# Queueing the transposes of a layer norm behind a later gather in a four-layer graph network kernel

## The chip, the cores and the metric

The kernel runs on one core of one Trainium2 chip. The metric is the device time in microseconds (us) of one execution. Before the change the median of three executions is 5404.78 us.

The engines are called by their short names: PE is TensorE (matmuls and transposes; PEld is its loading of weights), DVE is VectorE, ACT is ScalarE, POOL is GpSimd, SP is SyncE, which here issues DMAs.

## The reference, cut to what matters

There are 16 independent batches (graphs) of 1024 nodes with 128 features, and an adjacency matrix of 1024 x 1024 for each, about 1.6% of it filled plus the diagonal. Four layers follow each other. In front of each the features are normalised, and each adds its result to them:

```python
h = jnp.maximum(_layernorm(x, axis=-1), 0.0)
x = x + _L2_gnn_ref(h, adj, ...)          # layers 0, 1 and 3 in the same way
```

Layers 0 and 1 multiply the adjacency matrix with the features and a small weight. Layer 2 consists of two passes; each computes for every edge a score from the features of its two ends, forms messages from scores and adjacency, and updates the node features. Layer 3 is an attention with a softmax over the neighbours. The norm that the change is about is the one between layers 1 and 2: its result `h` is needed as it is (nodes on partitions, called `xf`) and transposed (features on partitions, called `xT`).

## The kernel before, in words

**Tiling.** The 1024 nodes are eight tiles of 128, so a batch's features are one SBUF tile of 128 x 8 x 128. Layer 2 works only on the existing edges. For each pair of node tiles (36 pairs: 28 off the diagonal, 8 on it) there are "hot" matrices of zeros and ones that pick a pair's edges out; off the diagonal they have 320 columns, on it 480. A *gather* is a product of such a matrix with the node terms: four matmuls into one PSUM bank `pre` (line 1008). ACT and DVE turn it into a hidden row `hid` (lines 1024 and 1025), *dots* reduce it to scores `sc` (line 1041), and *scatter* and *messages* bring them back to the nodes (lines 1098 to 1137). `pre` has two banks, so a gather has to wait until DVE has read the one before the last.

**Rounds.** One pass of layer 2 over a batch is a round. It goes through nine groups of four pairs: diagonal group 0, seven groups off the diagonal, diagonal group 8. The second round of a batch starts with the four diagonal gathers of group 0, while the second half of the node update of the first round is still under way (`between`, which calls `update`: matmuls h line 343 and xn line 352, transposes tx line 359, the add on DVE at line 360, statistics, a power on POOL, and from line 1170 the transposes and the `split` into the terms `part`, lines 297 and 892 to 894). Group 2's gathers are the first that need the second half's terms.

**Three lanes.** While the rounds of batch b run (lane m, the method `main`), the last part of batch b-1 (lane c, `last`: update and layer 3) and the first part of batch b+1 (lane a, `first`: layers 0 and 1, the norm of layer 2, then `build`, which makes the hot matrices) run beside them. Each lane is a generator. A `yield` names a cost in units of about a microsecond. `weave` (line 1264) keeps for each lane the sum of its yields divided by the lane's total (`MAIN_US`, `FIRST_US`, `LAST_US`), and always advances the lane that is furthest behind. What stands between two yields is traced in one piece.

**What sets the order.** This traced order is a priority. Tile's scheduler then simulates the engines with a cost model and gives each engine a fixed queue: of the instructions that are ready in the simulation, the one traced first goes next. An instruction that the simulation takes to be ready early can so be queued ahead of one traced earlier. On the chip each engine works through its queue in that order. `tc.issue_after(ins)` adds, to each instruction traced in its block on the engine of `ins`, an order behind `ins` in that queue, with no wait for the end of `ins`. The rounds already use it once, in `dots`.

**Around the change.** In `first`, after layer 1 has written the sum `x` (products nb line 289, then o and x, lines 330 to 335), `pre_ln` is called (line 776). Its `normal` takes statistics on DVE (bn, lines 231 to 239), the power on POOL (line 242), one more step on DVE (line 249), and then eight activations on ACT (line 251) that write `s.xf`. After a yield of 2, `transposed` puts eight transposes on PE (line 259), four into one PSUM bank, each four followed by a copy on ACT (line 260). Lane a has a single PSUM bank in these batches. After another yield of 2, `kept` writes `xT` and `x` to memory with DMAs on SP's queue (line 721), and `build` starts, whose first matmuls use the same bank. The lane's yields are, in order: 7.8 for layer 0's own terms, 32 for its eight tiles, 2 for the count, 22 for layer 1, the norm's 2 and 2, and 45.9 for `build`: 113.7 in all.

```python
yield from lane.pre_ln(xt, f"2_{name}", dst=s.xf)
s.xT = self.kept(lane.hT, "xT", f"xT0_{b}")
s.x = self.kept(xt, "x", f"xk_{b}")
yield from self.build(s, has, name)
```

Of the kernel before, what the change touches and what calls it, by code (L numbers as in the profile page):

```python
# [13 lines left out]
AF = mybir.ActivationFunctionType  # L14
# [26 lines left out]


MAIN_US = 184.0
FIRST_US = 115.0
LAST_US = 70.0


# [4 lines left out]
def tile_four_gnn_layers(  # L52
# [22 lines left out]
    nc = tc.nc  # L75
# [106 lines left out]
    def flat(t):  # L182
        return t.rearrange("p t d -> p (t d)")
# [346 lines left out]
    class Edges:  # L530
# [197 lines left out]
        def first(self, b):  # L728
            s = self.next = Batch()
            lane, name = self.a, f"{b}"  # L730
            xt = self.work.tile([P, T, D], F32, tag="x", name=f"x_{b}")
            nc.sync.dma_start(xt, x[b].rearrange("(t p) d -> p t d", p=P))
            for _ in lane.layer0_own(xt, name):
                if b:
                    yield 1.3
            z, own = lane.z, lane.o
            yield 0


            s.adjT = self.dram.tile([N, N], F32, tag="adjT", name=f"adjT_{b}", bufs=3)  # L740
            has = self.work.tile([P, len(BUCKETS), P], FP8, tag="has", name=f"has_{b}", bufs=1)
            deg = self.work.tile([P, 2, T], F32, tag="deg", name=f"deg_{b}")
            rdeg = deg[:, 1]
            for t in range(T):
                at = self.load(
                    "a", adj[b, t * P : (t + 1) * P, :].rearrange("p (k n) -> p k n", n=P),
                    f"at_{b}_{t}",
                )
                ct = self.load("a", self.columns(adj[b], t), f"ct_{b}_{t}")
                turned = lane.scratch(f"tn_{b}_{t}")  # L750
                nc.scalar.activation(turned, at, AF.Copy, accum_out=deg[:, 0, t : t + 1])
                for ks, ps in lane.halves(f"tn_{b}_{t}"):
                    for i, k in enumerate(ks):
                        nc.tensor.transpose(ps[:, i], at[:, k], ident)
                    nc.scalar.activation(turned[:, ks[0] : ks[-1] + 1], ps, AF.Copy)
                    yield 1
                nc.sync.dma_start(self.columns(s.adjT, t), turned)
                parts = [(INDEX[t, t], t, t + 1)]
                if t + 1 < T:
                    parts.append((INDEX[t, t + 1], t + 1, T))  # L760
                for i, lo, hi in parts:
                    nc.vector.tensor_tensor(
                        has[:, i : i + hi - lo], ct[:, lo:hi], turned[:, lo:hi],
                        op=OP.logical_or, saturate=False,
                    )
                nc.vector.reciprocal(rdeg[:, t : t + 1], deg[:, 0, t : t + 1])
                lane.layer0_tile(t, ct, z, own, rdeg, name)
                yield 2
            lane.layer0_end(xt, own)
            self.count(s, has, name)  # L770
            yield 2
            yield from lane.layer1(
                xt, lambda t: self.load("a", self.columns(s.adjT, t), f"l1_{b}_{t}"), rdeg, name
            )
            s.xf = self.work.tile([P, T, D], F32, tag="xf0", name=f"xf0_{b}", bufs=1)
            yield from lane.pre_ln(xt, f"2_{name}", dst=s.xf)
            s.xT = self.kept(lane.hT, "xT", f"xT0_{b}")
            s.x = self.kept(xt, "x", f"xk_{b}")
            yield from self.build(s, has, name)

# [175 lines left out]
        class Group:  # L956
# [41 lines left out]
            def gather(self, i):  # L998

                path, c = self.path, self.c  # L1000
                t, u = self.grp[i]
                on, om = self.s.on[t, u], self.s.om[t, u]
                for d in range(self.nd):
                    pre = path.m.one(f"pre_{self.name}_{i}_{d}")

                    for v, node, hot in ((d, t, on), (1 - d, u, om)):
                        for k in range(2):
                            nc.tensor.matmul(  # L1008
                                pre[:, :c], path.parts[node // Q][:, k, node % Q, v], hot[:, :c],
                                start=(hot is on and k == 0),  # L1010
                                stop=(hot is om and k == 1),
                            )
                    if not self.diag:
                        hid = path.work.tile(
                            [P, 2, C_OFF], F16, tag="hid", name=f"hid_{self.name}_{i}_{d}", bufs=N_HID
                        )
                    elif i % 2 == 0:
                        self.two = flat(path.m.scratch(f"hid_{self.name}_{i}")).bitcast(F16).rearrange(
                            "p (i v c) -> p i v c", i=2, v=2
                        )  # L1020
                        hid = self.two[:, 0]
                    else:
                        hid = self.two[:, 1]
                    nc.scalar.activation(hid[:, 0, :c], pre[:, :c], AF.Relu)  # L1024
                    nc.vector.scalar_tensor_tensor(  # L1025
                        hid[:, 1, :c], pre[:, :c], 0.0, hid[:, 0, :c], op0=OP.max, op1=OP.subtract
                    )
                    self.hid.append(hid)
                    yield 0.6
# [203 lines left out]
        def run(self):  # L1233


            self.alone(self.a, "amcam")
            first = self.first(0)
            next(first)
            self.scaled()
            for us in first:  # L1240
                if us is None:
                    break

            self.alone(self.a, "")
            self.a.banks = [self.own["c"], self.own["a"]]
            self.next.builds = first
            done = None
            for b in range(B):
                s = self.next
                lanes = [(self.main(s, b), MAIN_US)]  # L1250
                if b:
                    self.a.banks = [self.own["a"]]
                    lanes.append((self.last(done, b - 1), LAST_US))
                if b + 1 < B:
                    lanes.append((chain(s.builds, self.first(b + 1)), FIRST_US))
                else:
                    self.c.banks = [self.own["c"], self.own["a"]]
                self.weave(lanes)
                done = s
            self.alone(self.c, "cmamc")  # L1260
            for _ in self.last(done, B - 1):
                pass
# [123 lines left out]
    with ExitStack() as stack:  # L1386
        path = Edges(stack)
# [16 lines left out]
    with tc.If(full > 0):  # L1404
        with ExitStack() as stack:
            path = Pairs(stack)
# [36 lines left out]
```

## Time and profile before

| what | value |
|---|---|
| time, three executions | 5400.31, 5404.78, 5408.11 us |
| span of the profiled execution | 5411.4 us |
| busy PE, DVE, ACT, POOL | 5012.4, 4288.8, 3055.3, 176.5 us |
| mean granted clock of PE | 0.978 |
| HBM read and written | 446.44 and 100.66 MB |
| transposes of this norm (line 259, `tp<-ident,xf`) | 128, median 0.421 us |
| their activations (line 251, `xf<-x,st`) | 128, median 0.478 us |
| power of the norms on POOL (line 242, 128x8) | 64, median 1.636 us |

Busy time is what an engine spent inside instructions; the rest of the span it waited. The list of waits tells for each engine and line how long it stood idle before such instructions and which instruction of which engine ended that wait. A wait for several things is put down to the one that came last. The timeline lists instructions in order of time, and those that follow each other on one engine with the same line are merged. The windows give busy times and the granted clock of PE (1.00 is full speed) in stretches that one chooses.

From batch 2 on the periods are much alike: from one batch's transposes of this norm to the next one's it is 325 to 332 us.

### The profile page before, as it was taken

The numbers are of one execution on the slowest core, as the hardware profiler recorded it, in microseconds if no ns is written. First come the engines' busy times: TensorE is split into PE (matmuls) and PEld (weight loads), VectorE is DVE, ScalarE is ACT, GpSimd is POOL, SyncE is SP. The second block draws the span as 40 slices with busy tenths as digits, with TensorE's granted clock in tenths as the row PEclk, the third lists the DMA queues.
The fourth block names the chain that finished last, engine by engine and source line by source line (L and its number), as shares of the span: only waits on it lengthen the run. The fifth ranks groups of instructions, "written<-read, shape, count | busy, mean of one in ns | idle before, by whom it ended". The sixth has DMA issues, their size and how long they took to land.

```text
span 5411.4 us, 113484 instructions
## 1 busy us (share of the span) xinstructions
PE 5012.4 (93%) x45109; PEld 3743.8 (69%) x45109; DVE 4288.8 (79%) x10567; ACT 3055.3 (56%) x6790; POOL 176.5 (3%) x137
## 2 busy tenths in 40 slices
PE   5999999999999999999999999999999999999986
PEld 4666767767776767767777677677767677677664
DVE  4776787877879788797877878778797787978876
ACT  4556464655646556465565656556465564655533
POOL 0000000000000000000000000000000000000000
PEclk8999999999999999999999999999999999999998
DMA  6242425243252423424234242432424334243121
GB/s 182 66 138 87 120 60 150 79 128 103 76 149 64 136 92 99 133 67 124 92 112 121 61 142 87 122 106 76 147 67 137 91 96 136 67 128 92 53 62 47
DMA packets 740139, 554.56 MB, mean 102 GB/s; under 512 B 32272, under 2 KB 686352, under 8 KB 739600
## 3 DMA queue, kind: packets, MB, share of 16 engines
q1 hardware_dynamic: 734496, 545.58, 33.6%
q8 instruction: 356, 5.83, 0.5%
q10 hardware_dynamic: 5104, 1.65, 0.1%
q14 instruction: 183, 1.50, 0.1%
HBM read 446.44 MB, written 100.66 MB: 101 GB/s over the span
## 4 chain that ended last, share of the span: by engine, by line
PE 61%; DVE 20%; ACT 10%; DMA 4%; POOL 2%; issue 2%; SPq 0%; ACTq 0%; POOLq 0%; DVEq 0%
PE pre L1008 15%; PE p L1120 7%; DVE val L1098 6%; PE nb L289 6%; PE msg L1137 5%; PE h L343 4%; PE hp L507 3%; PE bb L297 3%; PE sc L1041 3%; DVE hid L1025 3%; DMA at<-in_adj_dram 3%; PE pq L865 2%; PE pn L829 2%; POOL st L242 2%; ACT hid L1024 2%
## 5 line engine op out<-in xcount | busy, mean ns | idle before, releaser
L1024 ACT ACTIVATE hid<-pre 128x320 f16<-128x320 f32 (+1 forms) x2048 | 922.2, 456 | 713.5 <-PE pre L1008 679.5
L1025 DVE SCALAR_TENSOR_TENSOR hid<-pre,hid 128x320 f16<-128x320 f32 (+1 forms) x2048 | 1010.0, 505 | 262.7 <-ACT hid L1024 245.8
L1008 PEld LDWEIGHTS <-part 128*128 128x128 f16 x8192 | 752.7, 99 | 429.3 <-issue 211.4
L1008 PE MATMUL pre<-on,part 128*128 128x320 fp8e4 (+1 forms) x4096 | 966.6, 311 | 42.5 <-DVE hid L1025 32.3
L1008 PE MATMUL pre<-om,part 128*128 128x320 fp8e4 (+1 forms) x4096 | 979.0, 312 | 0.0
L1098 DVE TENSOR_TENSOR val<-onT,u 128x384 f32<-128x384 fp8e4 (+1 forms) x1152 | 603.3, 580 | 3.6
L1137 PE MATMUL msg<-upd,xf 128*128 128x128 f32 (+3 forms) x3008 | 591.8, 320 | 0.0
L1120 PE MATMUL p<-val,omT 128*128 128x128 f16 x6528 | 532.7, 219 | 31.6 <-DVE val L1098 27.2
L1120 PEld LDWEIGHTS <-omT 128*128 128x128 fp8e4 x6528 | 433.4, 96 | 109.6 <-issue 37.1
L1098 DVE TENSOR_TENSOR val<-omT,u 128x384 f32<-128x384 fp8e4 x896 | 442.7, 549 | 0.0
L1137 PEld LDWEIGHTS msg<-upd,xf 128*128 128x128 f32 x3008 | 411.6, 191 | 17.6 <-DVE upd L1128 0.9
L877 ACT ACTIVATE om<-pm 128x320 fp8e4<-128x320 f32 (+1 forms) x576 | 268.6, 466 | 274.5 <-PE pm L829 270.1
L1128 DVE SCALAR_TENSOR_TENSOR upd<-p,adj 128x512 f32<-128x512 f32 x512 | 349.0, 682 | 80.7 <-PE p L1120 76.7
L1120 PE MATMUL p<-val,onT 128*128 128x128 f16 x4480 | 370.9, 220 | 1.4 <-DVE upd L1128 1.4
L861 ACT ACTIVATE onT<-pn 128x384 fp8e4<-128x384 f32 (+1 forms) x576 | 298.4, 518 | 106.4 <-PE pn L829 98.4
L1062 ACT ACTIVATE srow<-sc,be_s,down 128x128 f32<-128x128 f32 (+2 forms) x512 | 256.3, 540 | 163.3 <-PE sc L1041 162.3
L507 PE MATMUL hp<-wh,e 128*128 128x129 f32 x2048 | 331.1, 287 | 16.7 <-DVE e L503 16.7
L1120 PEld LDWEIGHTS <-onT 128*128 128x128 fp8e4 x4480 | 305.2, 97 | 49.5 <-issue 14.9
L507 PEld LDWEIGHTS hp<-wh,e 128*128 128x128 f32 x2048 | 279.9, 195 | 51.5 <-issue 24.0
L1041 PE MATMUL sc<-hid,slide 128*32 128x320 f16 (+1 forms) x4096 | 272.4, 320 | 29.9 <-DVE hid L1025 28.5
L820 DVE TENSOR_SCALAR on<-far,wid 128x384 fp8e4<-128x384 f16 (+1 forms) x576 | 238.6, 427 | 60.0 <-PE pre L1008 52.2
L816 ACT ACTIVATE far<-iota_off,mid 128x384 f16<-128x384 f16 x448 | 275.6, 629 | 11.8 <-DVE on L820 11.3
(217 smaller groups left out, 8122.0 us busy)
## 6 DMA issues: line engine op xcount, KB each, us to landing
at<-in_adj_dram SPq DMA_DIRECT2D x128, 512.0 KB, 4.1
ct<-in_adj_dram SPq DMA_DIRECT2D x128, 512.0 KB, 4.5
adjT<-tn SPq DMA_DIRECT2D x128, 512.0 KB, 5.3
l<-adjT SPq DMA_DIRECT2D x128, 512.0 KB, 4.3
adj<-adjT SPq DMA_DIRECT2D x256, 256.0 KB, 3.5
a<-adjT SPq DMA_DIRECT2D x128, 384.0 KB, 3.2
adj<-adjT SPq DMA_DIRECT2D x448, 64.0 KB, 2.2
adj<-adjT SPq DMA_DIRECT2D x192, 128.0 KB, 2.9
```

Of the source, the lines that this page charges most:

```text
L289: nc.tensor.matmul(ps, mat[:, k], z[:, k], start=(k == 0), stop=(k == T - 1))
L507: nc.tensor.matmul(sums[:, t], e[:, i, t * P : (t + 1) * P], wh[:, k + i, : D + 1], start=False, stop=True, skip_group_check=True,)
L816: nc.scalar.activation(far[:, : ck * P], self.iota[t == u][:, : ck * P], AF.Abs, bias=s.mid[:, i : i + 1])
L861: nc.scalar.activation(onT, pn[:, : ck * P], AF.Copy, saturate=False)
L1008: nc.tensor.matmul(pre[:, :c], path.parts[node // Q][:, k, node % Q, v], hot[:, :c], start=(hot is on and k == 0), stop=(hot is om and k = ...
L1024: nc.scalar.activation(hid[:, 0, :c], pre[:, :c], AF.Relu)
L1025: nc.vector.scalar_tensor_tensor(hid[:, 1, :c], pre[:, :c], 0.0, hid[:, 0, :c], op0=OP.max, op1=OP.subtract)
L1041: ins = nc.tensor.matmul(self.sc[g * G : (g + 1) * G, : self.c], self.path.slide[:, self.l, G - 1 - r : 2 * G - 1 - r], self.hid[self.done ...
L1098: nc.vector.tensor_tensor(pair[:, i % 2, :ck], right[:, :ck], v.to_broadcast([P, ck, P]), op=OP.mult)
L1120: nc.tensor.matmul(self.ps[d][:, i], left[:, k], halves[:, k, :, h], start=(k, h) == terms[0], stop=(k, h) == terms[-1],)
L1128: nc.vector.scalar_tensor_tensor(upd, self.ps[d], S_SCALE, self.adj[:, d * Q : (d + 1) * Q], op0=OP.add, op1=OP.mult,)
L1137: nc.tensor.matmul(self.msg[h][:, (lo - h * Q) * P : (hi - h * Q) * P], self.xf[mb // Q][:, mb % Q], up, start=False, stop=True, skip_grou ...
```

## The change

The call of `pre_ln` is written out as its two parts. The yield between the norm and its transposes is 5 in place of 2, and the lane's total `FIRST_US` is 118 in place of 115. For all batches but the first, the transposes are traced inside `tc.issue_after(self.gathered)`; `gathered` is the last matmul of the gather that has been traced last. The copies on ACT are traced in the same block, but only instructions on PE get the edge.

```diff
-FIRST_US = 115.0
+FIRST_US = 118.0
...
-            yield from lane.pre_ln(xt, f"2_{name}", dst=s.xf)
-            s.xT = self.kept(lane.hT, "xT", f"xT0_{b}")
+            lane.normal(xt, s.xf, AF.Relu, f"2_{name}")
+            yield 5
+
+            with ExitStack() as behind:
+                if b:
+                    behind.enter_context(tc.issue_after(self.gathered))
+                turned = lane.transposed(s.xf, f"2_{name}")
+            yield 2
+            s.xT = self.kept(turned, "xT", f"xT0_{b}")
...
-                            nc.tensor.matmul(
+                            ins = nc.tensor.matmul(
...
+                    path.gathered = ins.ins
```

## The prediction

> **What bounds the kernel now.** I read the page first: busy shares, then the clock row, then the chain.
>
> ```profile
> PE 5012.4 (93%) x45109; PEld 3743.8 (69%) x45109; DVE 4288.8 (79%) x10567; ACT 3055.3 (56%) x6790; POOL 176.5 (3%) x137
> PE 61%; DVE 20%; ACT 10%; DMA 4%; POOL 2%; issue 2%; SPq 0%; ACTq 0%; POOLq 0%; DVEq 0%
> ```
>
> TensorE (PE) is the bound, and time can only be won where it stands still or runs at a reduced clock. DVE is second. Next I read the list of waits, PE and DVE rows. Columns: total us, times, longest.
>
> ```profile
> PE tp L259 <- ACT xf L251: 38.5, 15, 5.0
> PE pre L1008 <- DVE hid L1025: 32.3, 51, 2.8
> PE sc L1041 <- DVE hid L1025: 28.5, 22, 1.8
> PE pre L1008 <- DVE part L894: 3.8, 15, 1.0
> DVE st L249 <- POOL st L242: 98.0, 63, 1.8
> ```
>
> The first row is the step that moves: 15 waits, of which one of 4.96 us is batch 0's, alone at the start, and 14 are of 2.39 to 2.40 us, one in each of batches 2 to 15 (batch 1 has none). 14 x 2.39 = 33.5 us. The timeline of batch 3 around one of them (start us, us, engine, line; in brackets idle before):
>
> ```profile
> 970.07 0.83 PE L507 MATMUL hp<-wh,e 128*128 128x129 f32 x6
> 971.67 0.43 PE L1008 MATMUL pre<-on,part 128*128 128x320 fp8e4 x2 [0.76 <-DVE hid L1025]
> 971.94 0.43 PE L1008 MATMUL pre<-om,part 128*128 128x320 fp8e4 x2
> 974.76 0.33 PE L259 MATMUL tp<-ident,xf 128*128 128x128 f32 x1 [2.39 <-ACT xf L251]
> 975.02 0.38 PE L1041 MATMUL sc<-hid,slide 128*32 128x480 f16 x2
> 975.33 0.33 PE L259 MATMUL tp<-ident,xf 128*128 128x128 f32 x1
> ...
> 974.01 0.17 DVE L249 SCALAR_TENSOR_TENSOR st<-st 128x8 f32<-128x8 f32 x1 [1.41 <-POOL st L242]
> 974.30 0.64 DVE L1025 SCALAR_TENSOR_TENSOR hid<-pre,hid 128x480 f16<-128x480 f32 x1
> ```
>
> See two things. PE waits 0.76 + 2.39 = 3.15 us in this stretch. And DVE is held too: L249 waits 1.41 us for the power on POOL, and the hidden row that the next scores (sc) need stands behind L249 on DVE and ends at 974.94. The transposes hide a second wait that ends 0.2 us later. The clock by single microseconds (PE, PEld, DVE, ACT, POOL busy, then PEclk):
>
> ```profile
> 974.00:975.00 1.00, 0.24 (x1) 0.14 (x1) 0.99 (x5) 0.79 (x3) 0.00 (x0) 1.00 0.00 0
> 977.00:978.00 1.00, 1.00 (x6) 0.54 (x5) 0.86 (x4) 1.00 (x4) 0.10 (x1) 0.50 0.02 8
> 979.00:980.00 1.00, 1.00 (x7) 1.00 (x5) 0.96 (x3) 0.41 (x1) 0.00 (x0) 0.50 0.63 191
> ```
>
> After the stop PE is at half clock for 3.4 us here; taken over 10 us windows around all 14 stops, the half-clock stretches add up to 75.1 us (eight stretches of 6.8 us, six of 3.4). At half clock the same work takes double, so they cost 37.5 us.
>
> **What the Trainium skill says.** "TensorE: Matmul & The Clock Gate", What's actually happening: the clock is halved after an idle window of about 3.4 us and comes back after a busy one. The trace agrees in size: halves come in steps of 3.4 us behind these stops, though the stop here is 3.15 us in two pieces. The same page, Architectural detail, says that ACT and DVE are strict first-in first-out and that PE only pulls weight loads ahead: so one unready transpose stops all matmuls behind it, and L249 stops the hidden row. The timeline shows both. I use no price from the skill.
>
> **The change, part by part.** No instruction is added or removed: 128 transposes (median 0.421 us in this place, 0.273 for the same form elsewhere), 32 copies, the same DMAs. What changes is the order in which the planner sees them.
>
> (a) The yield of 5 in place of 2 and FIRST_US 118 in place of 115. The first lane's total rises from 113.7 to 116.7, so its end stays where it was (0.989 of the batch both times). Adding the yields up to the norm gives 63.8: 63.8/115 = 0.555 of the batch before, 63.8/118 = 0.541 after. The last neighbour product (L289) goes from 0.537 to 0.524. The norm and all before it therefore come up to 1.4% of a batch sooner relative to the rounds: 0.014 x 327 us (the batch period in the windows between stops) = 4.6 us. The transposes are seen at 68.8/118 = 0.583 in place of 65.8/115 = 0.572, 3.6 us later.
>
> (b) The edge. At 0.583 the rounds have just issued the fourth diagonal gather of the second layer (0.578); before, it would have been the third (0.557). In the trace of before the transposes already come after the fourth (969.26) and one more (971.67). So the edge is a floor that keeps the planner from pulling the transposes up with the norm; by itself it does not move them down.
>
> What it gives: before 0.537 the last product waits behind the second diagonal gather and the update matmuls (h L343 1.88 us, gather 0.8, hp 0.7 in the PE timeline from 960.45 to 963.65); now it is seen ahead of them, so it can start some 3.2 us sooner. DVE has room: it is busy 0.22 to 0.48 of each microsecond from 962 to 966, and 1.00 from 968 on. Everything that hangs on it (o 1.24, x 1.22, bn 1.63, pow 1.64, ACT 0.50) moves with it, and the first transpose becomes ready near 974.7 - 3.2 = 971.5. PE is free from 970.9. The stop falls from 3.15 us to 0.6, and with a rest of the hidden-row wait I take 1.0. Bounds: 0 saved if the product cannot start sooner; 3.15 saved if all goes.
>
> Sum: 14 x 2.15 = 30 us of stop. Of the 37.5 us of half clock I take half, 19 us, since a stop of 1.0 us is well under a window but some batches lose the clock anyway (batch 1 does with 1.0 us of stop in the 5 us before its transposes). Together 49. Not all arrives at the end: between stops, the eight periods behind a 6.8 us half stretch average 328.7 us, the five behind 3.4 us 327.5; a difference of 1.2 for 1.7 us of lost PE work, so about 0.7 passes through. 0.7 x 49 = 34 us, 0.6%. Ceiling: 44.2 + 37.5 = 82 us, 0.7 of it 57, all of it 5329 in the profile.
>
> (c) The rest at nothing: the two copies (0.6 us) and the copy of xT to memory move later by 3 to 4 us. SyncE issues it at 980.21 and the next thing behind it that anyone needs soon is the load at 990.37; its reader is in the next batch. The single bank of lane a is held later, and the building of the hot matrices starts at 0.600 in place of 0.590; their readers are a batch away, and the lane's end is unmoved, which hides it. POOL has 3% of work.
>
> The profile's span, 5411.4, is 6.6 over the median 5404.78 of the timed runs (5400.31 to 5408.11). 5411.4 - 34 = 5377; against the median 5404.8 - 34 = **5370 us**.
>
> **The rivals.** *DVE's wait takes its place* (same). If the norm does not move up on DVE, L249 still waits 1.41 us for POOL, the hidden row still ends at 974.94, and PE waits for sc in place of the transpose: 0.2 us more of stop, then 0.4 saved because the scores are no longer paced by ACT. Within 5 us of 5404. For it: the two waits end 0.2 us apart. Against it: DVE stands idle from 964.5 to 965.6 in front of the chain.
>
> *The second half's update is pushed back* (slower). DVE's queue after the last product holds 1.24 + 1.22 + 1.63 + 0.6 us of the norm and a wait of 1.41. The add L360 (968.82) that heads the update of half 1 stands between them; it leads over xf, xfT (L1170), bb and part (L894, ending 989.4) to the gathers of group 2, and PE already waits for part 15 times, 3.8 us: no slack. If the norm's bn and L249 are now put ahead of L360, part comes up to 3.5 us later, in 14 batches 49 us, less the stop that is saved anyway (0.7 x 33): 5404 + 26 = 5430. It decides from the point where L360 starts after L249. For it: the norm is seen at 0.541, and the update's step that holds L360 at 0.552. Against: L360's input comes from PE at 968.7, after the moved bn would have run.
>
> *The edge and the pace do nothing to this stop* and only the new phase of lane a against the rounds counts: its transposes tn and products nb (L289), eight steps of each kind per layer, stand up to 1.4% of a batch elsewhere. Stops of PE elsewhere in a batch (0.5 to 1.5 us each, ten of them in batch 3) may go either way: 5404 plus or minus 15.
>
> **How the numbers follow.** Forecast 0.60, its own range 5340 to 5394 (ceiling with 0.8 passing through, down to a gain of 0.2%). DVE's wait instead 0.15, 5394 to 5416. Update pushed back 0.15, 5416 to 5450. Phase only 0.10, split 0.03 faster, 0.02 same, 0.05 slower. Faster 0.63, same 0.17, slower 0.20; 0.2% (11 us) is about what a measurement of this kernel can tell from no change. A range that leaves no more than 2 in 10 out takes the forecast's, the whole of the second case and part of the third: 5338 to 5425.
>
> **What would show it.** Right: the row of tp waiting for ACT xf falls from 38.5 us to under 15 (5 of them are batch 0's), half-clock stretches behind these places fall from 75 us to under 45, the last nb of layer 1 starts before the second diagonal gather, L249 ends before the fourth gather's hidden row. Wrong: PE waits for sc or pre on DVE hid grow by what tp loses (first rival), pre waits for part grow from 3.8 us (second), or the period between stops stays at 327 us with the stop gone (third).

## The result, and the profile after

The changed kernel takes **5337.48 us** (median of 4 executions, 5336.17 to 5341.52), where the kernel before takes 5403.35 in the same comparison: a ratio of 0.9879, 95% interval 0.9861 to 0.9896. That is 66 us less; 34 were forecast. The direction is right; the time lies half a microsecond below the predicted range. The profiled execution spans 5339.7 us, 71.7 less than that of before.

The page after, busy time by engine and then the chain that ended last by engine:

```profile
PE 4962.4 (93%) x45109; PEld 3720.1 (70%) x45109; DVE 4286.7 (80%) x10567; ACT 3065.2 (57%) x6790; POOL 176.5 (3%) x137
PE 58%; DVE 23%; ACT 10%; DMA 5%; POOL 2%; issue 2%; ACTq 0%; SPq 0%; POOLq 0%; DVEq 0%
```

The same 45109 matmuls keep PE busy 50.0 us less (5012.4 before), and PE's time outside them falls by 21.7 (399.0 to 377.3). DVE and ACT do the same work in the same time. Next the list of waits after (total us, times, longest); the lines have moved by 7 or 8, so L1015, L1033, L1049 and L901 are L1008, L1025, L1041 and L894 of before:

```profile
PE pre L1015 <- DVE hid L1033: 33.7, 68, 2.8
...
PE tp L259 <- ACT hT L260: 23.1, 14, 1.7
...
PE pq L872 <- ACT onT L868: 21.5, 57, 0.6
PE tp L259 <- ACT xf L251: 20.4, 15, 5.0
...
PE sc L1049 <- DVE hid L1033: 17.5, 21, 1.8
...
PE pre L1015 <- DVE part L901: 3.8, 15, 1.0
...
DVE st L249 <- POOL st L242: 74.6, 63, 1.8
```

The row that was to fall did fall, from 38.5 to 20.4 us, of which 5 are batch 0's. But a row is new that the transposes of before did not have at all: 14 waits for `hT`, the copy on ACT, up to 1.7 us each, 23.1 in all. Together the two make 43.5 us, so the stop has changed its name and not its size. The waits for the hidden row have not grown by it (pre 32.3 to 33.7, sc 28.5 to 17.5) and pre for part is unmoved at 3.8. The largest fall elsewhere is that of `pq` (a product in `build`), which in before waited 39.1 us for `onT`, up to 1.5 us at once.

The timeline after, batch 3, PE and then ACT and DVE (start us, us, engine, line; in brackets idle before):

```profile
956.08 1.95 PE L289 MATMUL nb<-z,l 128*128 128x128 f32 x16
...
959.58 0.57 PE L1015 MATMUL pre<-on,part 128*128 128x480 fp8e4 x2
...
965.29 0.57 PE L1015 MATMUL pre<-om,part 128*128 128x480 fp8e4 x2
966.96 0.33 PE L259 MATMUL tp<-ident,xf 128*128 128x128 f32 x1 [1.10 <-ACT xf L251]
...
968.50 0.43 PE L1015 MATMUL pre<-om,part 128*128 128x320 fp8e4 x2
970.59 0.55 PE L259 MATMUL tp<-ident,xf 128*128 128x128 f32 x3 [1.65 <-ACT hT L260]
971.70 0.88 PE L1049 MATMUL sc<-hid,slide 128*32 128x480 f16 x8 [0.57 <-DVE hid L1033]
...
966.41 3.18 ACT L251 ACTIVATE xf<-x,st 128x128 f32<-128x128 f32 x8 [1.55 <-DVE st L249]
969.50 0.55 ACT L1032 ACTIVATE hid<-pre 128x480 f16<-128x480 f32 x1
969.96 0.58 ACT L260 ACTIVATE hT<-tp 128x512 f32<-128x512 f32 x1
...
966.21 0.17 DVE L249 SCALAR_TENSOR_TENSOR st<-st 128x8 f32<-128x8 f32 x1 [1.11 <-POOL st L242]
966.30 0.65 DVE L1033 SCALAR_TENSOR_TENSOR hid<-pre,hid 128x480 f16<-128x480 f32 x1
```

The last product of layer 1 (956.08) does start ahead of the second diagonal gather (959.58), as predicted. The first transpose is ready 2.1 us after the start of the fourth diagonal gather (966.96 against 964.88), where it was 5.5 us after it before (974.76 against 969.26): 3.4 us nearer, and 3.2 were worked out. Yet the stop is now 1.10 + 1.65 + 0.57 = 3.32 us. The 1.65 us are spent on the lane's single bank: the first four transposes are done at 968.52, but their copy stands in ACT's queue behind activations 5 to 8 of `xf` and a hidden row. It starts at 969.96 and ends at 970.54, and only then may the second four start.

### The profile page after: what moved, and what is told of

Read it like the earlier page. It is cut to its first block, busy times and chain, and to the rows that moved or that the text cites. A ratio compares the mean times of both kernels' runs of the same rounds, so it can differ in the third digit from the quotient of the medians.

```text
span 5339.7 us, 113330 instructions
## 1 busy us (share of the span) xinstructions
PE 4962.4 (93%) x45109; PEld 3720.1 (70%) x45109; DVE 4286.7 (80%) x10567; ACT 3065.2 (57%) x6790; POOL 176.5 (3%) x137
## 3 DMA queue, kind: packets, MB, share of 16 engines
q10 hardware_dynamic: 5104, 1.65, 0.1%
## 4 chain that ended last, share of the span: by engine, by line
PE 58%; DVE 23%; ACT 10%; DMA 5%; POOL 2%; issue 2%; ACTq 0%; SPq 0%; POOLq 0%; DVEq 0%
PE pre L1015 15%; DVE val L1106 8%; PE p L1128 7%; PE nb L289 6%; PE msg L1145 5%; DMA at<-in_adj_dram 4%; PE sc L1049 3%; DVE hid L1033 3%; PE h L343 3%; PE bb L297 3%; PE pn L836 2%; PE hp L507 2%; PE pq L872 2%; ACT hid L1032 2%; POOL st L242 2%
## 5 line engine op out<-in xcount | busy, mean ns | idle before, releaser
L1033 DVE SCALAR_TENSOR_TENSOR hid<-pre,hid 128x320 f16<-128x320 f32 (+1 forms) x2048 | 1009.1, 505 | 232.9 <-ACT hid L1032 219.0
L1015 PEld LDWEIGHTS <-part 128*128 128x128 f16 x8192 | 748.3, 98 | 433.5 <-issue 210.4
L1015 PE MATMUL pre<-on,part 128*128 128x320 fp8e4 (+1 forms) x4096 | 971.8, 309 | 42.9 <-DVE hid L1033 33.7
L1015 PE MATMUL pre<-om,part 128*128 128x320 fp8e4 (+1 forms) x4096 | 972.7, 309 | 0.0
L1145 PEld LDWEIGHTS msg<-upd,xf 128*128 128x128 f32 x3008 | 406.5, 191 | 15.4 <-DVE upd L1136 1.7
L507 PEld LDWEIGHTS hp<-wh,e 128*128 128x128 f32 x2048 | 274.5, 195 | 36.6 <-DVE e L503 23.1
L876 DVE TENSOR_TENSOR omT<-pq,odd_off 128x384 fp8e4<-128x384 f32 x448 | 248.1, 554 | 55.6 <-PE pq L872 49.9
L1049 PE MATMUL sc<-hid,slide 128*32 128x320 f16 (+1 forms) x4096 | 269.6, 316 | 21.7 <-DVE hid L1033 17.5
L289 PE MATMUL nb<-z,ct 128*128 128x128 f32 x2048 | 267.6, 282 | 23.5 <-ACT tn L755 15.9
```

Of the source, the lines that this page charges most:

```text
L289: nc.tensor.matmul(ps, mat[:, k], z[:, k], start=(k == 0), stop=(k == T - 1))
L507: nc.tensor.matmul(sums[:, t], e[:, i, t * P : (t + 1) * P], wh[:, k + i, : D + 1], start=False, stop=True, skip_group_check=True,)
L1015: ins = nc.tensor.matmul(pre[:, :c], path.parts[node // Q][:, k, node % Q, v], hot[:, :c], start=(hot is on and k == 0), stop=(hot is om a ...
L1033: nc.vector.scalar_tensor_tensor(hid[:, 1, :c], pre[:, :c], 0.0, hid[:, 0, :c], op0=OP.max, op1=OP.subtract)
L1049: ins = nc.tensor.matmul(self.sc[g * G : (g + 1) * G, : self.c], self.path.slide[:, self.l, G - 1 - r : 2 * G - 1 - r], self.hid[self.done ...
L1145: nc.tensor.matmul(self.msg[h][:, (lo - h * Q) * P : (hi - h * Q) * P], self.xf[mb // Q][:, mb % Q], up, start=False, stop=True, skip_grou ...
```

## The experiments

All ratios are to the kernel before, run in the same comparison, with 95% intervals.

**The edge alone, the pace alone.** In `e2_no_edge` the edge is taken from the changed kernel. In `e1_pace_only` the yields of 2 and 5 are exchanged too, so that the norm comes as early as in the changed kernel and the transposes right behind it; FIRST_US stays 118 and `build` stays where the change put it.

```diff
-                if b:
+                if False:
```

and in e1 besides

```diff
-            yield 5
+            yield 2
...
-            yield 2
+            yield 5
             s.xT = self.kept(turned, "xT", f"xT0_{b}")
```

> Lane a's total is 118 and its yields add up to the same sum as in the changed kernel, but the 3 extra units stand after the transposes (norm, 2, transposes, 5) and there is no edge: the norm and all before it come sooner, the transposes do not come later. Theory P (the pace of lane a against the rounds makes the gain): ratio to before 0.988, half-clock time in the steady batches near the changed kernel's. Rival E (the transposes queued later make it): ratio 0.998 to 1.002 and the 2.4 us stop with its half clock is back.

> The changed kernel without the order behind the gather; yield of 5 and 118 kept. Theory P: ratio 0.988, since from batch 2 on the transposes come out behind the same gather anyway. Rival E: ratio 0.995 or more, as the transposes are pulled up to where ACT has not yet written their input.

Measured: e1 0.9858 (0.9838 to 0.9878), 5329.93 us; e2 0.985 (0.983 to 0.9871), 5327.21 us. The whole gain is there without the edge and without the later transposes. Compared as fixed queues, e2 differs from the changed kernel in batch 1 alone: from batch 2 on the edge orders nothing that the priorities did not order already. The edge alone, on the kernel before, was not run.

**The later transposes alone, the pace alone in its other half.** `e3_late_only` is the changed kernel with FIRST_US back at 115; `e4_first118` is the kernel before with 118.

```diff
-FIRST_US = 118.0
+FIRST_US = 115.0   # e3, on the changed kernel; e4 is the reverse, on the kernel before
```

> The changed kernel with the lane's total back at 115: the norm is traced at 0.555 of the batch as before the change, the transposes at 0.598 and with the edge. Theory P: ratio 0.997 to 1.003. Rival E: ratio 0.988 to 0.992.

> The kernel before with only the lane's total raised from 115 to 118; yields as before, so the lane's end comes at 0.964 of the batch in place of 0.989. Theory P: ratio 0.986 to 0.991, most of the gain from one number. Rival E: ratio 0.998 to 1.002. If what counts is that the lane's end stays at 0.989, the ratio is 0.995 or worse.

Measured: e3 0.9908 (0.9889 to 0.9926), 5357.4 us; e4 0.9914 (0.9895 to 0.9933), 5358.58 us. Each half gives some 0.9%, both together 1.2 to 1.5%. e3 lies in rival E's range and outside theory P's, e4 a hair above P's and outside E's: neither theory holds alone. In e3 the stop is a different one. Its timeline on PE:

```profile
965.17 0.43 PE L1015 MATMUL pre<-on,part 128*128 128x320 fp8e4 x2 [0.77 <-DVE hid L1033]
965.45 0.43 PE L1015 MATMUL pre<-om,part 128*128 128x320 fp8e4 x2
968.51 0.59 PE L1049 MATMUL sc<-hid,slide 128*32 128x480 f16 x8 [2.63 <-DVE hid L1033]
...
969.73 1.06 PE L259 MATMUL tp<-ident,xf 128*128 128x128 f32 x4
```

The transposes now wait for nothing, and PE waits 2.63 us for the hidden row that stands behind L249 on DVE. That is the mechanism of the first rival (the sc row goes from 28.5 to 63.1 us), and still the kernel is 48 us faster than before in the same comparison. The stop has changed hands there and hardly its length, so a shorter stop is not where the time comes from.

**Is it the wait for POOL?** If L249 is what holds DVE, DVE should not do it. In `e6_before_free_dve` (on the kernel before) and `e7_pace_free_dve` (on e1), DVE scales without waiting and POOL multiplies with its own power.

```diff
-            nc.vector.scalar_tensor_tensor(less, mean2, -0.5, rstd, op0=OP.mult, op1=OP.mult)
+            nc.vector.tensor_scalar(less, mean2, -0.5, None, op0=OP.mult)
+            nc.gpsimd.tensor_tensor(less, less, rstd, op=OP.mult)
```

> The kernel before, but the norm's last small step no longer waits on DVE for POOL's power: DVE scales the mean by -0.5 without waiting, and POOL multiplies it with the power; ACT then waits for POOL directly. Theory D (DVE held behind that step is the second lock of the stop, as seen by scores waiting for the hidden row): the DVE wait for POOL at that line (98 us) goes, but the transposes come later by POOL's second operation (about 1 us), so the stop before the transposes grows to 3 us or more; ratio 0.995 to 1.003. If the wait on DVE costs nothing: ratio 1.002 to 1.006.

> The pace-only kernel with the same freed DVE. Theory D: where the transposes are no longer last, freeing DVE pays: 2 to 5 us a batch less, ratio 0.978 to 0.984. If DVE's wait is hidden there: ratio 0.985 to 0.990.

Measured: 1.0006 (0.9997 to 1.0015) and 0.9857 (0.9841 to 0.9873), the latter against 0.9858 for e1. e6 lies in theory D's range, but e7 does not: freeing DVE pays nothing there either. In e6 PE still waits for `xf` 41.2 us (38.5 before): the chain to the transposes is no shorter.

**Is it the clock?** Fill matmuls on data that is ready when the stop begins stand ahead of the transposes in the kernel before (not in batch 0): they write a bank that the first transpose overwrites. One more line, not shown, keeps the variance that they read. Five, one, and two of them:

```diff
+                if h == 0 and b:
+                    for _ in range(N_FILL):
+                        nc.tensor.matmul(
+                            flat(ps)[:T], lane.var, flat(xt)[:, :HALF], start=True, stop=True
+                        )
                 for i, t in enumerate(ts):
                     nc.tensor.transpose(ps[:, i], s.xf[:, t], ident)
```

> The kernel before, with five more matmuls (8 columns of the norm's variance against 512 columns of x, into the bank that the first transposes then overwrite) queued right in front of the norm's transposes in batches 1 to 15. Their input is ready when the stop begins (variance written at 972.2 in batch 3, transposes start at 974.8), so they keep PE at work in the stop and shorten nothing. Theory C (more than half of the gain is the clock that is kept): half-clock time around the stops falls from 5.4 us a batch to under 2.5 and the ratio is 0.993 to 0.996. Rival (the gain is the idle time and the order, the clock is a by-product): ratio 0.999 or above, as the work only grows by about 2 us a batch.

> As the run with five filling matmuls, but with one (two halves of about 0.43 us each). From batch 2 on the queues of all engines are those of the kernel before, but for this matmul, which stands between the last gather and the transposes. It takes nothing off the stop: the transposes start when they did, only PE's longest idle stretch falls from 2.4 to 1.5 us. Theory C (the clock): half-clock time in the steady batches falls from 8.1 us to 3 to 6, and with 0.54 us of period per us of half clock (the slope between batches of the kernel before) the ratio is 0.9945 to 0.9985. Rival (idle time and order alone): ratio 0.9995 to 1.001.

> Two filling matmuls: the longest idle stretch falls to about 0.8 us. Theory C: half-clock time falls to 2 to 4 us a batch, ratio 0.992 to 0.996. Rival: ratio 1.000 to 1.002.

Measured: e5 0.9986 (0.9979 to 0.9993); e9 0.9988 (0.9982 to 0.9995); e10 0.9984 (0.9976 to 0.9991). All three lie between the ranges of the two theories. Five fills were too many: they ran 4.46 us, longer than the stop. For the clock, here are stretches of 2 us behind the stop, before and then e10, where the stop lies 3.0 us earlier (length, busy PE, PEld, DVE, ACT, POOL, then PEclk, DMA share, GB/s):

```profile
976.00:978.00 2.00, 2.00 (x11) 1.13 (x12) 1.10 (x5) 2.00 (x6) 1.10 (x1) 0.71 0.01 4
978.00:980.00 2.00, 2.00 (x11) 1.85 (x9) 1.97 (x6) 1.25 (x3) 0.00 (x0) 0.50 0.49 147
```

```profile
974.00:976.00 2.00, 2.00 (x15) 1.29 (x13) 1.87 (x7) 2.00 (x6) 0.09 (x1) 1.00 0.18 46
976.00:978.00 2.00, 1.20 (x15) 0.98 (x14) 1.97 (x6) 1.25 (x5) 0.00 (x0) 1.00 0.96 306
```

The half clock behind the stop is gone, in this batch and in the others: near the stop it is 5.36 us per batch before, 0.73 with one fill and none with two. Over whole batches, e9 and e10 have some 5 us less of it each, and e10's whole trace has as much half clock as the changed kernel's (154.4 us both, 241.6 before). That is worth 0.12 to 0.16%, 6 to 9 us. In the order of the kernel before, a kept clock is a real gain and a small one. The trace of e10 shows what holds it down:

```profile
977.01 0.66 PE L1185 MATMUL tp<-ident,xf 128*128 128x128 f32 x4 [0.80 <-DVE xf L374]
```

These are the transposes of the second half of the node update (L1170 before; L374 is the last step of that update on DVE, L371 before). With the clock kept PE comes to them sooner, but DVE ends the update when it did: 22.9 us after the start of the hidden row that opens the second round, in both kernels (means of the rounds of batches 2 to 14). So PE stands still for 0.80 us, and the transposes start at 22.9 where they started at 23.7. The fills therefore say what the clock is worth in the old order. What it is worth in the changed one, where DVE ends this update earlier, no run tests.

**Further along, and once more.** `e8_pace121` is e1 with 121 and a yield of 8 behind the transposes. `e11_pace_only_again` and `e12_changed_again` repeat e1 and the changed kernel in one comparison of five rounds.

> Pace only, one step further: lane total 121 and 8 units after the transposes. If an ever earlier lane a is better (trend): ratio 0.975 to 0.982. If 118 is one phase among several that avoid the long stop: ratio 0.984 to 0.994.

> The pace-only kernel once more beside the changed kernel on one chip. If the later queueing and the edge add nothing or cost a little: ratio 0.985 to 0.987, below that of the changed kernel by 0.001 to 0.003. If they help: above the changed kernel's.

> The changed kernel itself on the same chip as the others: ratio 0.987 to 0.989.

Measured: e8 0.9872 (0.9856 to 0.9889); e11 0.9867 (0.9852 to 0.9882), 5330.42 us; e12 0.9878 (0.9863 to 0.9893), 5337.36 us. The pace without the edge is as good as the change, and the better of the two each time by 7 to 8 us, though within the intervals.

**A scan of one number.** The kernel before with FIRST_US alone at 114, 116, 121 and 124.

```diff
-FIRST_US = 115.0
+FIRST_US = 114.0   # 116.0, 121.0, 124.0
```

> The kernel before with FIRST_US 114 alone: every step of lane a is seen up to 0.9% of a batch later against the rounds. Theory trend (earlier steps of lane a are better, 0.29% of time for each unit of FIRST_US, from 115 to 118): 1.003. Theory phase (the order of the queues at 115 happens to be a poor one, and neighbours of either side are better or like it without an order): 0.986 to 1.000, below 0.998 the likelier. A ratio above 1.001 speaks for the trend.

> The kernel before with FIRST_US 116 alone: steps of lane a up to 0.9% of a batch earlier. Theory trend: 0.997. Theory phase: no order, 0.988 to 1.004; a value at or below 0.991, a third of the way to 118 with all of its gain, speaks for the phase.

> The kernel before with FIRST_US 121 alone. Theory trend: 0.983, twice the gain of 118. Theory phase: 0.986 to 1.000, not better than 0.9914 of 118 by more than 0.004 except by chance, since the steady part of the gain of 118 came from one place behind the norm's stop (3.5 us per batch) that can't be won twice.

> The kernel before with FIRST_US 124 alone. Theory trend: 0.974. Theory phase: 0.986 to 1.002. A value above that of 118 contradicts the trend.

The table sets the scan beside the others. The last five columns are from the traces, in us per batch: the mean of 13 periods (from the end of this norm's transposes in batch 2 to their end in batch 15), PE's idle time and the half clock in it, and near these transposes the idle time (stretches that end between 4 us ahead of the first transpose and the end of the last: the stop) and the half clock (from 1 us ahead of the first to 5 us behind the last).

| kernel | ratio | period | PE idle | half clock | stop | half clock near it |
|---|---|---|---|---|---|---|
| FIRST_US 114 | 0.9986 (0.9976 to 0.9996) | 327.00 | 18.33 | 6.56 | 4.18 | 5.50 |
| before, 115 | 1 | 328.18 | 17.97 | 8.12 | 3.16 | 5.36 |
| 116 | 0.9954 (0.9937 to 0.997) | 326.34 | 17.08 | 3.41 | 2.09 | 1.95 |
| 118 (e4) | 0.9914 (0.9895 to 0.9933) | 325.01 | 17.88 | 2.10 | 2.30 | 1.69 |
| 121 | 0.993 (0.9913 to 0.9947) | 325.32 | 17.55 | 2.63 | 1.15 | 0.42 |
| 124 | 1.0153 (1.0132 to 1.0173) | 333.40 | 21.46 | 7.09 | 1.69 | 2.98 |
| changed, 118 | 0.9879 (0.9861 to 0.9896) | 323.29 | 16.50 | 2.17 | 3.32 | 2.19 |
| pace only, 118 (e1) | 0.9858 (0.9838 to 0.9878) | 322.87 | 16.41 | 2.10 | 2.30 | 1.85 |
| late only, 115 (e3) | 0.9908 (0.9889 to 0.9926) | 324.80 | 15.91 | 3.68 | 2.72 | 3.04 |

Read it against the stop. 121 has the smallest stop and almost no half clock near it, and is no faster than 118. 124 has about half the stop of before and is 1.5% slower. The changed kernel has the largest stop but one and the shortest time but one. The half clock alone does not order the kernels either: 118, the changed kernel and pace only have 2.1 to 2.2 us of it per period, and their periods lie 2.1 us apart. And FIRST_US has a valley rather than a slope, with its floor at 118 to 121: the trend's figures failed at 114, 121 and 124, and the phase's range held at 114, 116 and 121 and failed at 124. The waits of the kernel with 121 say the same in lines:

```profile
PE tp L259 <- ACT hT L260: 16.0, 14, 1.1
...
PE tp L259 <- ACT xf L251: 5.0, 1, 5.0
```

Only batch 0's wait for `xf` is left there (5.0, once): the row is where the prediction wanted it, and the time is 28 us above that of the changed kernel. With 124 other waits grow, from 32.3 and 15.4 us before:

```profile
PE pre L1008 <- DVE hid L1025: 56.5, 71, 2.9
PE pn L829 <- ACT om L877: 39.1, 97, 0.7
```

They are part of the 3.5 us by which PE's idle time per batch rises; why that order is so much worse was not followed further.

## Why the prediction was right and wrong

**What bounds it** held: time was won where PE stood still or ran slowly. **The move of the norm** held too, in place and in size (3.4 us nearer to its gather, 3.2 worked out), and so did the remark that the edge moves nothing down by itself: from batch 2 on it binds nothing.

**The step that failed is "the stop falls from 3.15 us to 1.0", the 14 x 2.15 = 30 us of the sum.** The stop is 3.32 us where it was 3.16, so this term gave nothing. The first transpose did come sooner, but the sum let all eight follow it. They go through one bank, so the second four wait for a copy that stands in ACT's queue behind the activations that feed them: 1.65 us that the waiting `xf` had covered before. Those parts, a single bank and one in-order queue, were named in the section on the kernel and never costed. The row of `xf` came to 20.4 us and not under 15. That the time fell all the same, by 66 us where 34 were forecast, is not this step's doing: for the larger part of the sum the direction came out right by luck.

**The clock** came out in length as forecast. Half clock behind these places falls from 5.36 to 2.19 us per batch, 75 to 31 us over 14 batches (under 45 was said), which is 22 us of lost work where 19 was taken. The prediction let 0.7 of that through, read from how periods and half clock go together between batches of one kernel. In the old order this is far too much: the fills give 6 to 9 us for some 5 us of half clock per batch, 13 batches long, or 32 us of lost work, a fifth to somewhat over a quarter. Over whole periods the change has 6.0 us less half clock (8.12 to 2.17). At the rate of the fills that would be 7 to 11 us of the 66; that the rate is the same in the new order is not shown.

**"The rest at nothing" failed as well.** That `build`'s readers are a batch away is true and beside the point, since its matmuls, copies and transfers stand in the same queues as the rounds. From e4 to e1 only three units of yield come in behind the transposes, so `build` and the writes start later: 0.9914 to 0.9858, 28.7 us.

**The update of the second half** was put at nothing in the forecast, and the second rival feared that it would come up to 3.5 us later. It came sooner. Here is DVE before and then after, from the add that heads this update (L360) to its last step (L371), with the statistics of the norm (bn):

```profile
968.82 0.68 DVE L360 TENSOR_TENSOR xf<-tx,xf 128x512 f32<-128x512 f32 x1
969.42 1.63 DVE L231 BATCH_NORM_STATS2 bn<-x 128x6 f32<-128x128 f32 x8
...
979.28 0.69 DVE L371 TENSOR_TENSOR xf<-xf,beta_bc 128x512 f32<-128x512 f32 x1
```

```profile
961.82 1.64 DVE L231 BATCH_NORM_STATS2 bn<-x 128x6 f32<-128x128 f32 x8
...
964.41 0.69 DVE L360 TENSOR_TENSOR xf<-tx,xf 128x512 f32<-128x512 f32 x1
...
972.57 0.68 DVE L371 TENSOR_TENSOR xf<-xf,beta_bc 128x512 f32<-128x512 f32 x1
```

Before, bn stands inside the update; after, it is done ahead of it, and the update takes 8.8 us in place of 11.2 in the mean. Counted from the start of the hidden row that opens the second round, it ends at 18.8 us and not 22.9. The reading on which that rival rested was wrong too: the 15 waits of `pre` for `part` (3.8 us) stand at the first gather of a batch (135.87 us, 797.35 us and so on), ahead of its first round, and none of them behind this update.

**The third rival came nearest**, with a size of plus or minus 15 us and a chance of 0.10, both far too small. FIRST_US alone, on an unchanged list of instructions, moves the time from 47 us below (118) to 78 us above (124). Before, at 115, stood on the poor side of a valley. The first two rivals fell: the hidden row took the stop's place only in e3, which is faster than before all the same, and the update was not pushed back.

**Where the time went,** in so far as it can be told: of the 71.7 us between the spans, 13 periods that are 4.89 us shorter make 63.6. Of the 4.89, PE's idle time gives 1.47, none of it at the stop; its largest item is `pq`'s wait for `onT` (39.1 to 21.5 us in the whole trace). The other 3.42 are a PE that is busy for less time with the same matmuls. On paper 2.98 of them, half of the 5.95 us of half clock that are gone, are the clock (43.6 of the 50.0 us in the whole trace), though the fills got only a part of such a sum.

The hidden rows of the gathers show where the two kernels part: up to the first row of group 1 in the second round they are level (176.5 and 176.0 us from the batch's first), by the first of group 2 the changed kernel is 4.6 us ahead (198.5 and 193.9), and at the end of the batch 4.9. So the gain is made right behind the old stop, where the update ends. The runs fit an account with two limits that lay 0.8 us apart: PE, held by the stop and the half clock, came to the update's transposes at 23.7 us, and DVE was done with the update at 22.9. e9 and e10 move the first alone and gain 0.7 and 0.8 us there; e6 moves the second alone, to 21.2, PE comes at 23.4, and the time is unchanged. The changed kernel moves both, to 19.4 and 18.8. But this is argued and not tested, and it can't be all: in e3 the two stay at 23.3 and 23.1 and it is 0.9% faster, and with 124 the update ends at 16.6 and the kernel is slower. The other lanes' work in that stretch is not the same either (16 of `build`'s `pq` matmuls before, 8 after), so work has moved out of it as well as waits.

How the 4.9 us divide between the clock, the earlier update and the work that moved stays **open**. What the runs show is that the new order of the queues makes the gain, and that a shorter stop, the edge, DVE's wait for POOL or, in the old order, the clock does not make it alone.

## What to carry to other kernels

Where two streams are interleaved by a planner and the engine that bounds them is 93% busy, the largest stop at one place is a poor forecast of what moving that place is worth: the move shifts everything else in the stream, and here such a shift alone was worth from -0.9% to +1.5%. Scan the planner's phase first, one number at a time, and compare a clever ordering with the best of the scan and not with the one value that happened to be there. When a wait is shortened, list what becomes ready next in each in-order queue, above all where one buffer is used twice: the second use waits next. And where two limits lie close together, as PE and DVE did here at the update, moving one of them alone shows little: look for the second before the first is called worthless.

## What the hardware showed that was not expected

In the order of the kernel before, half clock cost less than the half of its length that it takes from PE. The Trainium skill ("TensorE: Matmul & The Clock Gate", What's actually happening) states the halving behind idle time, and the traces agree that a stop of some 3 us, in two or three pieces, has half clock behind it (0.50 in the stretch from 978 to 980 us) and that work in the stop prevents it. But two fills that kept the clock at 1.00 behind the stop gained 0.16% (0.09 to 0.24), where some 0.6% was lost on paper (5 us of half clock, 2.5 us of work, in a batch that takes 328 us, is 0.76%, in 13 of 16 batches). The matmuls at full clock only brought PE sooner to a result that DVE had not finished, and PE waited 0.80 us for it.
